# Later LSTM weights fetched and summed eight gates behind a change of phase, and a group's second output one gate later

## The chip, the cores and the metric

The kernel runs as one launch on one core of a Trainium2 chip. The metric is the device time of one execution in microseconds, given as the median of several runs. Beside it stands a profile of one execution, with every engine's instructions and every DMA.

## The reference, cut to what matters

The program has four layers on x of 128 × 64 × 256 float32, which is 8192 tokens of 256 features. Each layer is normalised first (layer norm, then ReLU) and added to its input. The change lies in layer 0, which runs two graph convolutions and then an LSTM over windows of p = 1, 2, 3 and 4 neighbouring nodes, each p with weights of its own:

```python
for p in range(1, MAX_SKIP + 1):
    nw = Tv // p
    wins = h[:, :nw * p, :].reshape(Bv * nw, p, Hd)
    last = _lstm_last(Wih[p - 1], Whh[p - 1], bih[p - 1], bhh[p - 1], wins)
    idx = jnp.arange(nw) * p + (p - 1)
    h = h.at[:, idx, :].set(last.reshape(Bv, nw, Hd))
# _lstm_last, one step:
g = x_t @ Wih.T + h @ Whh.T + bias
i, f, gg, o = jnp.split(g, 4, axis=-1)
c = sigmoid(f) * c + sigmoid(i) * tanh(gg)
h = sigmoid(o) * tanh(c)
```

The window p + 1 reads what the window p has written. Layer 1 (attention over the edges of a graph) takes the sum of x and layer 0's output; layers 2 and 3 follow.

## The kernel before

**Groups, halves, phases.** The 8192 tokens are four groups g = 0 to 3 of 2048. A group's hidden state lies feature-major in SBUF in `hTs0[g % 2]`, so two groups are there at once: half 0 is groups 0 and 1, half 1 is groups 2 and 3, whose states wait in DRAM (`hmem`, in the trace `hm8` to `hm15`, chunks of 512 tokens). For each half the windows w = 1 to 4 run in turn. That makes eight phases (0 to 7), of 12, 28, 22 and 30 gates per half, 184 gates in all. The loop at L820 to L882 goes over these gates, one "slot" each.

**A gate.** A product of a gate's weights with the inputs (and, from the second step of a window on, with the hidden state) is computed with seven instead of eight block products, in the manner of Strassen. This needs sums of weight blocks and sums of input blocks. `Weights` (L424) fetches one window's `Wih` or `Whh` by a DMA on SP's queue (1 MB) and forms its sums by four `tensor_tensor` on GpSimd (L440, tiles `sih` and `shh`). The `ih` weights have two buffers, the `hh` weights one. `prepare` (L617) forms the sums of inputs in tile `xop`: on VectorE L623, L628 and L629 for w = 1; on ACT L632 and L633 and on VectorE L634, L640 and L641 for the other windows.

`gate` (L686) is a generator that gives TensorE the products in four parts. The PSUM tiles are `pa` (three buffers), `pc` (three) and `pb`, which takes one of the two buffers named `bank`. Three gates are interleaved: in a slot TensorE runs products 1 and 2 of the new gate, 3 and 4 of the gate two slots older, 5 of the last one, and 6 and 7 of the new one. VectorE adds the products together at L695 (`pb`), L710 (`pc` of the oldest) and L705 (`pa` of the last gate), in the order in which they are written; product 3 of a gate waits for the L705 of the same gate. `gate_done` follows with the element-wise LSTM (L728, L729, L737, L750 and their neighbours).

**At the change of a phase.** The loop calls `phase_over(ph)` (L806) two slots behind the last gate of phase `ph`. It creates the next phase's `hh` weights at once, if there are any to be used (w = 1 has none), and puts the `ih` weights of phase `ph + 2`, which take the buffer that has just come free, on the list `later_weights` with a due slot eight gates later. When that slot comes, L865 creates them.

**Program order and the scheduler.** The order of instructions on an engine isn't only the order in which the program is written: a scheduler may move an instruction ahead of others on its queue when nothing binds it. `late` (L71) calls `tc.keep_in_program_order` and pins an instruction behind everything written before it on that engine. The weights of L865 aren't pinned in this kernel, so that their DMA and sums are moved up to the change of phase itself: the trace has eight sums in a row there, four `sih` and four `shh`, with the `ih` fetch ahead of the `hh` fetch.

**Output of a group.** When the last step of w = 4 of a group is done, its output is due in two parts, c = 0 and c = 1 (L882). `group_out(g, c)` (L779) transposes 2 × 512 tokens on TensorE (L167, 16 transposes into the two `bank` buffers), adds them to x in tile `xres` on VectorE (L172, four adds), stores the two chunks of the sum by DMAs on GpSimd's queue (`xa`), and for the first half reloads the freed part of `hTs0` with the other half's state from `hmem` by SP (L789). x itself has been fetched by `fetch_x` on SP (`xres` from x). It is called in the part of the loop that runs only when there is a new gate; what is still due behind the last gate goes into `last_outs` (L883). Layer 1 then fetches the x chunks for what is left in `last_outs` (L919), behind the DMAs of its own first weights (`wlv`, L914 to L916, and `wout`), and `edges(q)` (L1281) calls one `group_out` in each of its first steps.

**Layer 2's weights** (`layer2_weights`, L927) are fetched during layer 1: `w1T` by SP and its sums by GpSimd in `quarter_sums` (L126), beside the layer norms of layer 1, whose roots (L99 to L102) also run on GpSimd and whose scaling (L109) runs on ACT.

Of the kernel before, what the change touches and what calls it, by code (L numbers as in the profile page):

```python
# [13 lines left out]
ALU = mybir.AluOpType  # L14
# [3 lines left out]
T = 64  # L18
# [12 lines left out]
def gnn_stack_kernel(ctx: ExitStack, tc: tile.TileContext, a: dict, out: bass.AP):  # L31
    nc = tc.nc
# [45 lines left out]
    class Norm:  # L78


        def __init__(self, xt, root_on_scalar=False, keep=late):
            self.xt, self.root_on_scalar, self.keep, self.h = xt, root_on_scalar, keep, None
            self.st = stat.tile([P, 4, 6], F32, tag="ln_st", name="ln_st")
            self.mv = stat.tile([P, 4, 2], F32, tag="ln_mv", name="ln_mv")
# [170 lines left out]
    keep = tabs.tile([P, E], F32, tag="keep", name="keep")  # L255
# [159 lines left out]
    with ExitStack() as l0:  # L415
# [6 lines left out]


        class Weights:  # L424
            def __init__(self, kind, w):
                bufs = 2 if kind == "ih" else 1
                t = wsp.tile([P, 2, 4, 2, P], F32, tag=f"w{kind}", name=f"w{kind}", bufs=bufs)
                s = wsp.tile([P, 3, 4, P], F32, tag=f"s{kind}", name=f"s{kind}", bufs=bufs)
                nc.sync.dma_start(
                    out=t.rearrange("p k q j m -> p k (q j m)"), in_=a[f"W{kind}T"][:, w - 1]  # L430
                )
                a11, a12, a21, a22 = t[:, 0, :, 0, :], t[:, 1, :, 0, :], t[:, 0, :, 1, :], t[:, 1, :, 1, :]
                s1, s2, s4 = s[:, 0], s[:, 1], s[:, 2]
                for o, x, y, op in (
                    (s1, a21, a22, ALU.add),
                    (s2, s1, a11, ALU.subtract),
                    (s4, a12, s2, ALU.subtract),
                    (a21, a11, a21, ALU.subtract),
                ):
                    nc.gpsimd.tensor_tensor(o, x, y, op)  # L440
                self.of = {1: a11, 2: a12, 3: s4, 4: a22, 5: s1, 6: s2, 7: a21}

            def __call__(self, k, q):
# [6 lines left out]
        weights = {}  # L450


        with ExitStack() as conv:
# [43 lines left out]
            p = bank()  # L497
# [97 lines left out]
        class Step:  # L595
# [21 lines left out]
            def prepare(self):  # L617

                N, t = self.N, self.t
                x = xop.tile([P, 7 * NMAX], F32, tag="x", name="xop")  # L620
                if self.w == 1:
                    v = x[:, : 4 * N].rearrange("p (q n) -> p q n", n=N)
                    nc.vector.tensor_tensor(  # L623
                        v[:, 0:2], self.nodes(slice(2, 4), 0), self.nodes(slice(0, 3, 2), 0), ALU.subtract
                    )
                    b11, b21, b22 = (self.nodes(slice(k, k + 1), 0)[:, 0] for k in (0, 1, 3))
                    nc.vector.tensor_tensor(v[:, 2], b22, v[:, 0], ALU.subtract)
                    nc.vector.tensor_tensor(v[:, 3], b21, v[:, 2], ALU.subtract)  # L628
                    self.x = {1: b11, 2: b21, 3: b22, 4: v[:, 3], 5: v[:, 0], 6: v[:, 2], 7: v[:, 1]}  # L629
                    return  # L630
                v = x[:, : 7 * N].rearrange("p (q n) -> p q n", n=N)
                nc.scalar.copy(self.as_nodes(v[:, 0:2]), self.nodes(slice(0, 2), t))  # L632
                nc.scalar.copy(self.as_nodes(v[:, 2:3]), self.nodes(slice(3, 4), t))  # L633
                nc.vector.tensor_tensor(  # L634
                    self.as_nodes(v[:, 3:5]),
                    self.nodes(slice(2, 4), t),
                    self.nodes(slice(0, 3, 2), t),
                    ALU.subtract,
                )
                nc.vector.tensor_tensor(v[:, 5], v[:, 2], v[:, 3], ALU.subtract)  # L640
                nc.vector.tensor_tensor(v[:, 6], v[:, 1], v[:, 5], ALU.subtract)  # L641
                self.x = {1: v[:, 0], 2: v[:, 1], 3: v[:, 2], 4: v[:, 6], 5: v[:, 3], 6: v[:, 5], 7: v[:, 4]}

            def product(self, q, targets):
# [112 lines left out]
        steps, phases = [], []  # L757
        for half in range(2):
            ga, gb = 2 * half, 2 * half + 1
            for w in range(1, MAX_SKIP + 1):  # L760
                ph = len(phases)
# [55 lines left out]
        later, outs = [], []  # L817
        norm_steps = iter(())
        steps[0].prepare()
        for slot in range(len(tasks) + 2):  # L820
            new = tasks[slot] if slot < len(tasks) else None
            if slot == len(tasks):

                for _ in norm_steps:
                    pass
                first_hT = gp.tile([P, 4 * NMAX], F32, tag="gate", name="hT1_first")
                first_hT = first_hT[:, : 2 * CHUNK].rearrange("p (c t) -> p c t", c=2)
                for ip in range(2):
                    transpose_features(norms1[0].h, first_hT, ip, late)
            if new:  # L830
                step = steps[new[0]]
                one = step.gate(new[1])
                next(one)
            if len(flight) > 1:
                old = flight.pop(0)
                next(old[1], None)
                next(flight[-1][1])
            elif flight and not new:
                old = flight.pop(0)
                next(old[1], None)  # L840
            else:
                old = None
                if flight:
                    next(flight[-1][1])
            if new:
                next(one)
                flight.append((new, one))
                at, k = new[0], new[2]
                while outs and outs[0][0] <= slot:
                    group_out(*outs.pop(0)[1:])  # L850

                new_half = at + 1 < len(steps) and at and steps[at + 1].w == 1 < step.w
                if k == len(step.gates) - (1 if new_half else 2) and at + 1 < len(steps):
                    steps[at + 1].prepare()
                if step.w == MAX_SKIP and step.t == 2 and k < 2 and step.g < NGR - 1:
                    for u in range(2):
                        n = 4 * step.g + 2 * u + k
                        later.append((slot, "x", n))
            while later and later[0][0] <= slot:
                _, kind, n = later.pop(0)  # L860
                residual[n] = fetch_x(n)
            next(norm_steps, None)
            while later_weights and later_weights[0][0] <= slot:
                _, ph = later_weights.pop(0)
                weights["ih", ph] = Weights("ih", phases[ph])  # L865
            if old:
                (at, q, k), step = old[0], steps[old[0][0]]
                if k == len(step.gates) - 1:
                    if at + 1 == len(steps) or steps[at + 1].phase != step.phase:
                        phase_over(step.phase)  # L870
                    if step.phase == len(phases) - 1 and step.t == 1 and step.g == NGR - 1:

                        t_ = wsp.tile([P, 2, 4, 2, P], F32, tag="wih", name="x_first", bufs=2)
                        flat = t_.rearrange("p k q j m -> p k (q j m)")
                        norms1 = {}
                        for n in range(2):
                            xt = flat[:, n, :].rearrange("p (i d) -> p i d", i=4)
                            nc.sync.dma_start(out=xt, in_=xa[n])
                            norms1[n] = Norm(xt)
                        norm_steps = first_norms1(norms1)  # L880
                    if step.w == MAX_SKIP and step.t == MAX_SKIP - 1:
                        outs += [(slot + 1, step.g, 0), (slot + 2, step.g, 1)]  # L882
        last_outs = [(g, c) for _, g, c in outs]  # L883
    psums["banks"] = None

# [2 lines left out]
    with ExitStack() as l1:  # L888
# [306 lines left out]
        def sums(n, xt, keep=False):  # L1195

            st = stat.tile([P, 4, 6], F32, tag="ln_st", name="ln_st")
            mv = stat.tile([P, 4, 2], F32, tag="ln_mv", name="ln_mv")
            for i in range(4):
                ins = nc.vector.bn_stats(st[:, i, :], xt[:, i, :])  # L1200
                if keep and i == 0:
                    late(ins)
                nc.vector.bn_aggr(mv[:, i, :], st[:, i, :])
            rs, nm = w12t["x_rs"][:, n, :], w12t["x_nm"][:, n, :]
            ins = nc.gpsimd.tensor_scalar(rs, mv[:, :, 1], 1e-5, None, ALU.add)
            if keep:
                late(ins)
            nc.gpsimd.tensor_tensor(rs, rs, half_power, ALU.pow)
            nc.gpsimd.tensor_tensor(nm, mv[:, :, 0], rs, ALU.mult)
            nc.gpsimd.tensor_scalar(nm, nm, -1.0, None, ALU.mult)  # L1210
# [158 lines left out]
    with ExitStack() as l2:  # L1369
# [273 lines left out]
        for k in range(2):  # L1643
            f = t4.tile([P, 4, P], F32, tag=f"field{k}", name=f"field{k}", bufs=1)
# [348 lines left out]
```

## Time and profile before

| | |
|---|---|
| median of three runs | 2067.21 us (2066.95 to 2071.63) |
| the profiled execution, its own time | 2061.03 us |
| its span | 2059.3 us |
| mean granted TensorE clock | 0.996 |
| graph convolutions of layer 0 | up to about 190 us |
| LSTM | about 190 to 1273 us |
| layer 1 | about 1273 to 1660 us |
| GpSimd's weight sums in the LSTM (stretches) | 273.4–279.5, 408.5–422.6, 560.8–573.8, 742.4–752.5, 817.45–822.6, 953.9–967.9, 1107.1–1112.5 us |
| a group's outputs | about 724–757 (groups 0 and 1), 1257–1267 (group 2), behind 1273 (group 3) |

Two kinds of view are used below. In a table of windows each row is a stretch of the span: its bounds, its length, then for each engine its busy time and in brackets how many instructions it has run, at the end TensorE's granted clock (1.00 is full speed), the share of the time in which the DMA engines were busy, and the rate of transfer. In a timeline each row is one instruction or a few equal ones in a row: start in us, duration, engine, line of the program, operation, output and inputs with their shapes, and in brackets how long the engine had been idle before it and what released it. PEld is the load of weights into TensorE, which overlaps with its matmuls. The times of the profiled execution are from the start of its span; its own time is 6.2 us (0.3%) under the median of the runs.

### The profile page before, as it was taken

The page shows a single profiled execution, that of the slowest core. Times are in us where ns is not written, and L with a number is a line of the kernel's source. Part 1 is how long each engine was busy: PE and PEld are TensorE (multiplying, and loading weights), DVE is VectorE, ACT ScalarE, POOL GpSimd, SP SyncE. Part 2 cuts the span into 40 slices and gives each one's busy share as a digit, 9 for nine tenths or more (in the row PEclk, how much of TensorE's full clock was granted, in tenths as well). Part 3 has the DMA queues.
Part 4 walks back from the last instruction along what each step waited for, and adds up shares of the span by engine and source line. Part 5 has one row for each costly group of instructions (what it writes and reads, how often), then busy time and mean ns, then how long its engine had stood idle before and what let it go on. Part 6 is the DMA issues. An engine that isn't in the chain of part 4 may idle for free. (4 is left out here: it accounts for less than half of the span.)

```text
span 2059.3 us, 25491 instructions
## 1 busy us (share of the span) xinstructions
PE 2006.1 (97%) x9444; PEld 1346.1 (65%) x9444; DVE 1359.5 (66%) x2507; ACT 1184.4 (58%) x2230; POOL 308.2 (15%) x416
## 2 busy tenths in 40 slices
PE   8999999999999999999999999999999999999998
PEld 6777478866688845887667887333334775444786
DVE  8755666564565477566556555677777877886776
ACT  4344766555565457566446564666675556591544
POOL 3000010020110020002001000323223420000563
PEclk9999999999999999999999999999999999999999
DMA  9331000100100170001001003412223841022012
GB/s 316 98 98 51 0 21 1 42 0 1 41 1 1 40 246 21 1 0 42 0 1 41 1 16 120 138 61 97 72 98 122 298 154 52 0 82 82 32 62 72
DMA packets 63196, 135.06 MB, mean 66 GB/s; under 512 B 6240, under 2 KB 40928, under 8 KB 60768
## 3 DMA queue, kind: packets, MB, share of 16 engines
q1 hardware_dynamic: 56832, 109.11, 15.6%
q0 software_dynamic: 5632, 24.12, 3.1%
q8 instruction: 74, 1.21, 0.2%
q14 instruction: 50, 0.41, 0.1%
q10 hardware_dynamic: 608, 0.20, 0.0%
HBM read 87.28 MB, written 46.14 MB: 65 GB/s over the span
## 5 line engine op out<-in xcount | busy, mean ns | idle before, releaser
L651 PE MATMUL pa<-xop,sih 128*128 128x256 f32 (+2 forms) x1056 | 344.4, 418 | 11.7 <-DVE gate L705 8.2
L679 ACT ACTIVATE gate<-gate,bias 128x256 f32<-128x256 f32 (+2 forms) x368 | 247.4, 679 | 173.6 <-DVE gate L695 91.0
L651 PEld LDWEIGHTS pa<-xop,sih 128*128 128x128 f32 x1056 | 198.4, 190 | 87.9 <-issue 22.8
L651 PE MATMUL pc<-xop,wih 128*128 128x256 f32 (+2 forms) x736 | 251.2, 423 | 0.0
L695 DVE TENSOR_TENSOR gate<-pb,gate 128x256 f32<-128x256 f32 (+2 forms) x184 | 87.5, 475 | 225.7 <-PE pb L651 154.1
L651 PE MATMUL pa<-lstm_h,shh 128*128 128x256 f32 (+1 forms) x672 | 212.7, 398 | 0.0
L993 DVE SCALAR_TENSOR_TENSOR lr<-lr 128x1024 f32<-128x1024 f32 x128 | 151.1, 1222 | 55.3 <-ACT lr L992 55.3
L651 PEld LDWEIGHTS pc<-xop,wih 128*128 128x128 f32 x736 | 139.8, 190 | 51.2 <-issue 23.0
L710 DVE TENSOR_TENSOR gate<-pc,gate 128x256 f32<-128x256 f32 (+2 forms) x184 | 87.6, 476 | 121.2 <-PE pc L651 120.9
L992 ACT COPY lr<-pair 128x1024 f32<-128x1024 f32 x128 | 123.1, 1014 | 47.6 <-PE pair L986 47.6
L651 PEld LDWEIGHTS pa<-lstm_h,shh 128*128 128x128 f32 x672 | 127.7, 190 | 30.2
L651 PE MATMUL pc<-lstm_h,whh 128*128 128x256 f32 (+1 forms) x448 | 141.8, 398 | 0.0
L694 ACT COPY gate<-pa 128x256 f32<-128x256 f32 (+2 forms) x184 | 76.1, 413 | 96.7 <-PE pa L651 96.1
L986 PE MATMUL pair<-sd_hot,xq 64*128 64x512 f32 x512 | 127.5, 616 | 0.3 <-ACT lr L992 0.3
L705 DVE TENSOR_TENSOR gate<-pa,gate 128x256 f32<-128x256 f32 (+2 forms) x184 | 87.5, 475 | 44.0 <-PE pa L651 43.4
L970 PE MATMUL bank<-wlv,hT 128*128 128x512 f32 x240 | 110.7, 604 | 0.0
L699 ACT COPY gate<-pa 128x256 f32<-128x256 f32 (+2 forms) x184 | 75.4, 410 | 59.1 <-PE pa L651 57.9
L679 ACT ACTIVATE gate<-pa,bias 128x256 f32<-128x256 f32 (+2 forms) x184 | 94.0, 511 | 23.6 <-PE pa L651 22.0
L440 POOL TENSOR_TENSOR sih<-wih 128x512 f32<-128x512 f32 x8 | 10.7, 1335 | 630.6 <-DMA wih<-in_WihT 484.4
L651 PE MATMUL pa<-xop,wih 128*128 128x256 f32 (+1 forms) x320 | 101.4, 398 | 2.7 <-ACT xop L632 2.7
L651 PE MATMUL pb<-xop,wih 128*128 128x256 f32 (+1 forms) x320 | 100.3, 398 | 0.4 <-DVE gate L695 0.4
L651 PEld LDWEIGHTS pc<-lstm_h,whh 128*128 128x128 f32 x448 | 85.1, 190 | 20.1
(346 smaller groups left out, 3809.2 us busy)
## 6 DMA issues: line engine op xcount, KB each, us to landing
field<-sd_hot SPq DMA_DIRECT2D x4, 2304.0 KB, 17.2
wih<-in_WihT SPq DMA_DIRECT2D x8, 1024.0 KB, 5.1
xres<-in_x SPq DMA_DIRECT2D x16, 512.0 KB, 4.6
xa<-xres POOLq DMA_DIRECT2D x16, 512.0 KB, 5.2
dense<-field POOLq DMA_DIRECT2D x4, 2048.0 KB, 8.5
xin<-xb SPq DMA_DIRECT2D x16, 512.0 KB, 3.4
h<-xb SPq DMA_DIRECT2D x16, 512.0 KB, 3.2
xin<-in_x SPq DMA_DIRECT2D x15, 512.0 KB, 3.9
```

The costliest lines, as they stand in the source:

```text
L440: nc.gpsimd.tensor_tensor(o, x, y, op)
L651: ins = nc.tensor.matmul(p[:, : self.N], weights[kind, self.phase](k, q), x[k], start=first_ and kind == "ih", stop=kind == "hh" or not se ...
L679: nc.scalar.activation(out, in_, AF.Tanh if q == 2 else AF.Sigmoid, bias=bias[:, self.w - 1, 2 * q + j : 2 * q + j + 1],)
L694: nc.scalar.copy(blk[0, 0], pa[:, :N])
L695: nc.vector.tensor_tensor(blk[0, 0], pb[:, :N], blk[0, 0], ALU.add)
L699: nc.scalar.copy(blk[1, 0], pa[:, :N])
L705: nc.vector.tensor_tensor(blk[1, 1], pa[:, :N], blk[1, 1], ALU.add)
L710: nc.vector.tensor_tensor(blk[1, 0], pc[:, :N], blk[1, 0], ALU.add)
L970: ins = nc.tensor.matmul(p, hTs[n][:, k, i * P : (i + 1) * P], wlv[:, k, :], start=k == 0, stop=k == 1)
L986: ins = nc.tensor.matmul(p[:, par, :], queries[it][r, c * P : (c + 1) * P], sd_hot[r, :], start=True, stop=True)
L992: nc.scalar.copy(lr, p)
L993: nc.vector.scalar_tensor_tensor(lr, lr, 0.2, lr, ALU.mult, ALU.max)
```

## The change

The diff, with the alias in `prepare` (`copy, sums = nc.scalar.copy, nc.vector.tensor_tensor`, used for the same five calls in the same order) left out:

```diff
         class Weights:
-            def __init__(self, kind, w):
+            def __init__(self, kind, w, keep=lambda ins: None):
...
-                nc.sync.dma_start(
-                    out=t.rearrange("p k q j m -> p k (q j m)"), in_=a[f"W{kind}T"][:, w - 1]
+                keep(
+                    nc.sync.dma_start(
+                        out=t.rearrange("p k q j m -> p k (q j m)"), in_=a[f"W{kind}T"][:, w - 1]
+                    )
                 )
...
-                    nc.gpsimd.tensor_tensor(o, x, y, op)
+                    keep(nc.gpsimd.tensor_tensor(o, x, y, op))
...
                 _, ph = later_weights.pop(0)
-                weights["ih", ph] = Weights("ih", phases[ph])
+                weights["ih", ph] = Weights("ih", phases[ph], late)
...
                     if step.w == MAX_SKIP and step.t == MAX_SKIP - 1:
-                        outs += [(slot + 1, step.g, 0), (slot + 2, step.g, 1)]
+                        outs += [(slot + 1, step.g, 0), (slot + 3, step.g, 1)]
```

First, the `ih` weights that L865 creates are pinned where the program has them: their SP DMA and their four GpSimd sums stand eight gates behind `phase_over`. Six sets are concerned, those of phases 2 to 7; the weights of phases 0 and 1 and all `hh` weights are as before. Nothing is added or dropped in number: 24 sums and 6 DMAs change places. At each change of phase the `hh` fetch and its sums come first now.

Second, a group's second output is due three slots behind its last gate's completion instead of two. For group 0 its transposes move behind the first gate of the new half, its adds on VectorE behind L729 and ahead of L628; with them move its two stores and its reload of `hTs0`. For group 1 they move by one gate, the adds behind L737 and L623. For group 2 the due slot falls behind the last new gate, so that this output stays in `last_outs` with the two of group 3: three calls of `group_out` are left for layer 1 instead of two, at q = 0, 1 and 2, and group 3's two come one step later each. Its two chunks of x are fetched again at L919 (SP's fetches into `xres` go from 16 to 18).

The order of the queues changes around this: the two fetches of x into `xres` that wait for stores of group 2's first output stand ahead of `wlv` and `wout` on SP; `w1T` of layer 2 stands behind a load of layer 1's input and is created behind one more output; its GpSimd sums stand ahead of and among the roots (L99, L100) of the norm for chunk 3.

## The prediction

> **What bounds the kernel.** The page's first part comes first: TensorE is busy for 97% of the span. I then cut the LSTM stretch into windows and read TensorE's idle time as length less busy time.
>
> ```profile
> PE 2006.1 (97%) x9444; PEld 1346.1 (65%) x9444; DVE 1359.5 (66%) x2507; ACT 1184.4 (58%) x2230; POOL 308.2 (15%) x416
> ...
> 285.00:404.00 119.00, 118.94 (x547) 103.56 (x547) 67.53 (x127) 71.45 (x152) 0.00 (x0) 1.00 0.00 1
> 404.00:428.00 24.00, 21.82 (x76) 13.79 (x75) 21.61 (x33) 17.52 (x32) 13.92 (x8) 1.00 0.23 88
> 556.00:580.00 24.00, 19.72 (x85) 15.28 (x85) 21.70 (x36) 16.95 (x33) 12.82 (x8) 1.00 0.23 88
> 712.00:736.00 24.00, 20.55 (x89) 14.45 (x88) 13.85 (x21) 7.68 (x15) 2.38 (x4) 0.93 0.77 246
> 736.00:765.00 29.00, 27.85 (x92) 14.33 (x91) 21.80 (x29) 17.82 (x27) 12.06 (x12) 1.00 0.70 246
> 810.00:830.00 20.00, 18.23 (x78) 13.94 (x77) 18.44 (x36) 16.29 (x35) 5.05 (x4) 1.00 0.16 53
> 949.00:974.00 25.00, 22.83 (x80) 14.42 (x79) 22.42 (x34) 18.43 (x33) 13.85 (x8) 1.00 0.22 85
> 1101.00:1121.00 20.00, 17.20 (x76) 13.51 (x75) 18.12 (x34) 15.31 (x31) 5.33 (x4) 1.00 0.28 106
> 1255.00:1320.00 65.00, 63.43 (x304) 33.49 (x305) 42.22 (x63) 34.40 (x58) 16.28 (x22) 1.00 0.56 192
> ```
>
> Columns: stretch, its length, busy time of PE, PEld, DVE, ACT, POOL, granted clock, DMA share, GB/s. Inside a phase (row 285:404) TensorE idles 0.06 us of 119 and VectorE works 57%. The idle time sits at the changes of phase, of half, and of layer: 2.18, 4.28, 3.45, 1.15, 1.77, 2.17, 2.80, 1.57 us in the eight rows below. With 0.86 at 268:285 that is 20.2 us, the most this change could touch. Who ends each wait, from the timeline (start, length of one, engine, line, tiles, count, idle before and its releaser):
>
> ```profile
> 713.28 2.16 SPq L789 DMA_DIRECT2D hT<-hm  x2
> ...
> 720.61 1.23 DVE L623 TENSOR_TENSOR xop<-hT 128x1024 f32<-128x1024 f32 x1 [3.48 <-DMA hT<-hm]
> ...
> 724.89 1.25 PE L167 MATMUL bank<-ident,hT 128*128 128x128 f32 x8 [3.10 <-DVE xres L172]
> ...
> 756.05 1.25 PE L167 MATMUL bank<-ident,hT 128*128 128x128 f32 x8 [0.80 <-DVE xres L172]
> ...
> 570.55 2.10 DVE L634 TENSOR_TENSOR xop<-hT 128x512 f32<-128x512 f32 x1
> ...
> 824.91 0.68 DVE L634 TENSOR_TENSOR xop<-hT 128x512 f32<-128x512 f32 x1
> ...
> 971.63 0.83 PE L651 MATMUL pa<-xop,sih 128*128 128x336 f32 x2 [1.56 <-DVE gate L705]
> ```
>
> Two different things are to be seen. An output's transposes (L167) wait at 724.89 for VectorE's adds (L172) to free one of two banks. And the same L634 takes 2.10 us while GpSimd sums weights, 0.68 us when it does not.
>
> **A. Second output of group 0, one gate later.** Before: 3.27 us of stall at 724.89, then 3.40 us (726.2 to 729.6) at a granted clock of 0.51, whose work at full clock would take 1.73, so 1.67 more: 4.9 in all. After: the transposes stand behind the new half's first gate; VectorE's four adds then queue behind two L728/L729 operations of about 1.22 each, so the third bank comes about 1.65 late (0.5 to 3). The output also issues the half's last reload of hT. Issued near 730.7 and landing 5.6 later as the row at 713.28 did (waited for until 720.61, plus store time), it comes at 736.3; VectorE's L623 wants it near 733.7, and behind L623 queue L695, L710, L705, which TensorE waits for. L705 then ends about 738.6, wanted at 738.4: +0.2 (0 to 3). Gain 4.9 − 1.65 − 0.2 ≈ **−3.1** (−4.5 to +1).
>
> Here a rule is weighed. The Trainium skill, "TensorE: Matmul & The Clock Gate", section on the HAM clock gate, has the array slow down after a fully idle window of roughly 3.4 us that runs free, so an idle of 3.10 need not cool it; by the rule alone only 3.27 would be won and A is −1.4. The row shows a clock of 0.51 directly behind the 3.10; I take the row. If the new 1.65 stall cooled it too, A would be about −1.4 again; no 1.5 us stall elsewhere did (clock 1.00 at 556:580).
>
> **B. Second output of group 1.** Before 0.80 at 756.05. After, its adds stand behind L737 and L623 on VectorE (1.2 each): stall ≈ 2.3, **+1.5** (−0.8 to +2).
>
> **C. Groups 2 and 3.** Group 2's second output falls due after the last gate, so it is left over: it runs in layer 1, and so do group 3's two, each one step later. Away go stalls at the LSTM's end, 2.83 us of transposes with their waits (1264.21 to 1267.04) and 0.59 at 1271.47; added in layer 1: 16 transposes at the rate there, 2.2 (1.9 to 2.4). **−1.2.** Its two 512 KB chunks of x are fetched again.
>
> **D. SP's queue at the layer change.** Two x fetches that wait for stores of group 2 now stand ahead of the layer's first weights (before: issued at 1227). The store at 1257.90 let its fetch go at 1260.98, the second at 1262.55; so the weights go at about 1263.1 and 1263.7 and land at an estimated 1268.5 to 1269.3 (wih took 5.1 for 1 MB; these are half that or less each, behind 1 MB of x). Their first user in before:
>
> ```profile
> 1273.30 3.60 PE L970 MATMUL bank<-wlv,hT_first 128*128 128x512 f32 x8
> ```
>
> About 3 us of transposes ahead of it are gone, so it wants them near 1270: **+0.3** (0 to 2.5). Layer 2's w1 now goes later too, about 1304 for 1295.94, and GpSimd's sum of it stands ahead of a norm's roots (L99); the norm's scaling on ACT comes about 1 us late against a slack of 0.35 in front of TensorE's pair bank: **+0.7** (0 to 2.5).
>
> **E. Weight fetch and sums leave the phase changes.** Six groups of one 1 MB fetch and four GpSimd sums (1.27 us each) go to the eighth gate behind; none is added. What disappears is counted from windows with and without them.
> - 810:830 holds four of the moved sums alone: L641 at 817.59 took 1.41 us beside a sum and 0.42 without, and 0.9 of the stall goes.
> - 404:428 and 949:974 hold eight (four moved, four of whh that stay and now come first): the waits of .38/.39 and 1.73 end on operations stretched by the moved ones, −1.8 each with the first .55 staying.
> - 556:580 (eight) becomes like 1101:1121 (four of whh alone): 4.28 to 2.80, taken as −1.0, because there the remaining four still meet L634.
> - 268, 736 and 1101: nothing.
>
> Sum **−5.5** (−3 to −7).
>
> The second rule speaks against this. The Trainium skill, "SBUF — State Buffer", section "Who interferes with whom", has certain VectorE instructions with two SBUF inputs and a GpSimd instruction exclude each other for whole instructions. The trace agrees: L634 2.10 = 0.70 + about 1.40, operations with a PSUM input (L695, L705: 0.41) unchanged. So moving removes no collision: by the rule four sums of 1.28 put up to 5.1 us on VectorE wherever they land, six groups 30.7 us. What decides is VectorE's slack there: 43% in row 285:404. The nearest row for landing is 736:765, eight sums at 742 to 752, where VectorE's operations were not longer and TensorE's only stall among them was the .51 that steps always have. I take 0.15 a group, **+0.9** (0 to 12.7, rival 3).
>
> **Sum.** −3.1 + 1.5 − 1.2 + 0.3 + 0.7 − 5.5 + 0.9 = −6.4 us on the profiled execution's 2061.03 (span 2059.3). The median of the runs, 2067.21, lies 6.2 above it, so the saving is set against the median: **2060.8 us**, −0.31%. A measurement of this kernel tells about 0.3% (6.2 us) from no change, so the forecast lies on that border.
>
> **Rivals.**
> 1. *The reload, the layer weights or w1 take A and C back.* DMA is at 0.77 in 712:736, and three chains have under 1 us of slack by my working; against it, each has a landing row that just fits. A, B, C, D then give 0 together, E and its landing −4.6: 2062.6. If all of that and half of E fails: 2065.
> 2. *The sums cost as much where they land.* For it: the exclusion rule and the stall of 1.73 at 971.63. Against it: VectorE's slack there. E and landing 0, the rest −1.8: 2065.4.
> 3. *Slower.* The landing gate is one where L641/L634 stand directly ahead of L705, so each of six groups costs what 964.71 and 971.63 did together, .39 + 1.73 = 2.1. Then +12.7 − 5.5 − 1.8 = +5.4: 2072.6. It decides from 1.2 us a group ((5.5 + 1.8)/6). Against it beside the slack: only one gate in 3 or 4 prepares a new step, and a group's sums (5 us) cover less than one gate (184 gates in some 1083 us, 5.9 each).
> 4. *All of it pays.* A 4.9 without a new stall, E 7, landing free: −12, 2055.
> 5. *It does not do what it says.* For the third group this is so already: its output is not one gate later but in another layer, with x fetched twice; counted in C and D.
>
> **Chances.** Forecast case (2058 to 2062) 0.37; rival 4 and its neighbourhood 0.18; rival 1 0.18; rival 2 0.14; rival 3 0.13. Faster by over 0.3% (under 2061.0): most of rival 4, two thirds of the forecast, a little of rival 1, 0.50. Within: 0.37. Slower: 0.13. Range 2054.5 to 2069.
>
> **What would show it.** After: at 712:736 a clock of 1.00 and no L167 wait over 2 us; L623 of the new half waiting under 1 us on hT; the four sih sums some ten gates behind each phase change, and TensorE's idle time in that window within 0.3 us of row 285:404; 810:830 under 1 us idle, 404:428 and 949:974 near 0.5; L970's first matmul not waiting for wlv. Wrong if any moved group costs TensorE over 1.2 us, if a stall over 2.5 us stands on hT, wlv or xres, or if the clock falls at another place.

## The result and the profile after

The median is 2072.53 us for the changed kernel against 2070.03 us for the kernel before, 17 runs each; the ratio is 1.0011, with a 95% interval from 1.0004 to 1.0017. So the change costs 2.3 us or 0.1%, where 6.4 us less were forecast. In a second measurement the ratio was 1.0014 (1.0007 to 1.0020), so that the loss is small, but both intervals lie above 1. One run of the changed kernel, 2140.17 us at a mean clock of 0.944, is left out of the ratio. The forecast of 2060.8 stood on a median of 2067.21 from three runs of the kernel before; its 17 runs here give 2070.03, so 2.8 us of the distance from 2060.8 to 2072.53 are not the change's. The profiled execution took 2073.39 us, with a span of 2071.6.

The table of windows after, in the columns of the one shown before:

```profile
404.00:428.00 24.00, 21.54 (x75) 13.60 (x74) 21.74 (x32) 17.21 (x31) 13.56 (x8) 1.00 0.23 88
556.00:580.00 24.00, 19.60 (x84) 15.13 (x83) 21.68 (x35) 16.43 (x33) 13.45 (x8) 1.00 0.23 88
712.00:740.00 28.00, 25.07 (x103) 17.21 (x102) 16.81 (x25) 10.09 (x20) 2.39 (x4) 0.94 0.65 217
740.00:770.00 30.00, 27.85 (x88) 13.76 (x87) 22.44 (x30) 17.67 (x27) 7.10 (x8) 1.00 0.63 217
810.00:830.00 20.00, 18.47 (x78) 13.95 (x77) 18.44 (x34) 16.33 (x32) 5.11 (x4) 1.00 0.15 53
949.00:975.00 26.00, 23.83 (x85) 15.37 (x84) 23.09 (x36) 18.96 (x34) 13.84 (x8) 1.00 0.21 82
1101.00:1121.00 20.00, 17.02 (x73) 13.14 (x72) 18.09 (x31) 14.61 (x28) 5.25 (x4) 1.00 0.28 106
1255.00:1320.00 65.00, 63.86 (x307) 34.24 (x305) 41.34 (x63) 31.81 (x54) 14.13 (x22) 1.00 0.54 182
1320.00:1326.00 6.00, 3.47 (x12) 1.19 (x8) 3.26 (x6) 4.48 (x7) 0.00 (x0) 0.72 0.69 261
```

The fifth figure with its count is GpSimd. There are still eight sums at 404:428, 556:580 and 949:975, and four at 810:830: **five of the six sets that were to move have not left the changes of phase.** TensorE's idle time there is 2.46, 4.40, 2.17 and 1.53 us, for 2.18, 4.28, 2.17 and 1.77 before. The last row is new: 2.53 us of idle time in layer 1 and a granted clock of 0.72. Before, there was nothing:

```profile
1320.00:1326.00 6.00, 6.00 (x24) 2.87 (x22) 5.16 (x10) 3.73 (x7) 0.04 (x1) 1.00 0.06 24
```

The timeline of the changed kernel at the first of these changes of phase (L442 is L440 of the kernel before, L637 is L634, L708 is L705):

```profile
409.22 1.28 POOL L442 TENSOR_TENSOR shh<-whh 128x512 f32<-128x512 f32 x1 [129.60 <-DMA whh<-in_WhhT]
...
414.41 2.59 POOL L442 TENSOR_TENSOR sih<-wih 128x512 f32<-128x512 f32 x1
...
417.15 2.17 DVE L637 TENSOR_TENSOR xop<-hT 128x672 f32<-128x672 f32 x1
...
420.44 2.58 POOL L442 TENSOR_TENSOR wih<-wih 128x512 f32<-128x512 f32 x1
...
426.71 0.83 PE L654 MATMUL pa<-xop,sih 128*128 128x336 f32 x2 [1.56 <-DVE gate L708]
```

The same place before:

```profile
416.73 2.17 DVE L634 TENSOR_TENSOR xop<-hT 128x672 f32<-128x672 f32 x1
...
426.29 0.83 PE L651 MATMUL pa<-xop,sih 128*128 128x336 f32 x2 [1.56 <-DVE gate L705]
```

The four of whh come first, as the new order says. The four of wih follow at once and stretch L637 to 2.17 us, as those of whh, which came last before, did with L634; the stall of 1.56 is there to the hundredth. GpSimd had been idle for 129.60 us: with nothing on its queue that could hold it, a pinned operation runs as soon as its weights land. The pin says behind what it stands on its own queue, and the gates that it was meant to trail run on other engines. So the early start needs no moving by the scheduler, to which the text on the kernel before puts it down.

The exception is the change of half. There the pinned fetch stands on SP's queue behind two reloads of hT that wait themselves (L792), so it is issued at 765.21 (736.90 before), and the sums run from 774.50 (742.42 before):

```profile
761.58 3.58 SPq L792 DMA_DIRECT2D hT<-hm  x2
765.21 0.88 SPq L430 DMA_DIRECT2D wih<-in_WihT  x1
...
774.50 1.27 POOL L442 TENSOR_TENSOR sih<-wih 128x512 f32<-128x512 f32 x1 [7.99 <-DMA wih<-in_WihT]
```

TensorE idles for 0.00 us from 773 to 784. Here something ahead on the same queue did take time, and the pin did delay.

A stage-by-stage account needs one more view, of the change and of the experiments that follow. Each row takes the same operation (the nth L705 of the gates, the nth L993 of layer 1's edges) in two traces and gives how much later it starts than in the profile of before.

| us later than before at | 626 | 693 | 793 | 940 | 1271 (LSTM's end) | 1312 | 1328 | 1562 |
|---|---|---|---|---|---|---|---|---|
| change, first profile | 0.55 | 0.55 | 1.71 | 1.21 | −1.66 | 0.89 | 5.10 | 5.10 |
| change, second profile | 1.39 | 1.39 | 0.22 | −0.01 | −3.07 | −0.51 | 0.61 | 0.61 |
| pin only | 0.44 | 0.44 | −0.10 | −0.23 | −0.14 | −0.14 | −0.14 | −0.14 |
| later output only | −0.67 | −0.67 | 2.64 | 2.52 | −0.78 | 1.77 | 2.89 | 2.89 |
| later output, groups 0 and 1 | −0.14 | −0.14 | 1.09 | 1.08 | 1.26 | 1.26 | 1.26 | 1.26 |
| held sums, eight gates | −4.79 | −4.79 | −3.57 | −3.36 | −5.38 | −5.38 | −5.38 | −5.38 |
| change, w1's sums behind the norm | 0.70 | 0.70 | −0.50 | −0.80 | −3.47 | −0.91 | −0.91 | −0.91 |
| the same, and held | −3.96 | −3.96 | −3.98 | −3.70 | −8.71 | −6.15 | −6.15 | −6.15 |
| held, third group alone later | −4.56 | −4.56 | −4.32 | −4.08 | −9.04 | −6.49 | −6.49 | −6.49 |
| group 0 alone later | −0.50 | −0.49 | 0.43 | 0.49 | 0.23 | 0.22 | 0.23 | 0.23 |
| held sums, three gates | 10.89 | 10.89 | 11.06 | 16.08 | 19.66 | 19.66 | 19.66 | 19.66 |
| before, second profile | 1.45 | 1.45 | 1.25 | 1.24 | 0.40 | 0.40 | 0.40 | 0.40 |

The last row says how finely it can be read: the kernel before differs from itself by 1.7 us at 303, ahead of the changes of phase, and by up to 0.8 between columns. The change's first profile loses at three places: the change of half (693 to 793), the third output in layer 1 (1271 to 1312: 2.55), and 1312 to 1328 (4.21). It wins 3.0 at the LSTM's end.

The half's change, in the timeline of the changed kernel (L731 and L732 are L728 and L729 of before):

```profile
728.07 1.23 DVE L731 TENSOR_TENSOR gate<-gate,lstm_c 128x1024 f32<-128x1024 f32 x1 [1.10 <-ACT gate L682]
729.33 1.23 DVE L732 TENSOR_TENSOR lstm_c<-gate 128x1024 f32<-128x1024 f32 x1
...
731.21 1.59 PE L167 MATMUL bank<-ident,hT 128*128 128x128 f32 x8 [2.34 <-DVE xres L172]
...
763.35 1.26 PE L167 MATMUL bank<-ident,hT 128*128 128x128 f32 x8 [1.80 <-DVE xres L172]
```

The adds stand behind L731 and L732 as forecast, but L731 itself waited 1.10 us for ACT, so that the stall is 2.34 us and not 1.65. And 1312 to 1328:

```profile
1305.83 0.34 SPq L934 DMA_DIRECT2D w1T<-in_W1T  x1
...
1313.45 1.27 POOL L136 TENSOR_TENSOR w1S<-w1T 128x256 f32<-128x256 f32 x1 [5.74 <-DMA w1T<-in_W1T]
...
1314.81 1.08 POOL L99 TENSOR_SCALAR ln_rs<-ln_mv 128x4 f32<-128x4 f32 x1
...
1317.92 1.05 POOL L100 TENSOR_TENSOR ln_rs<-ln_rs,half_power 128x4 f32<-128x4 f32 x1
...
1319.60 2.07 ACT L109 ACTIVATE h<-xin,ln_nm,ln_rs 128x256 f32<-128x256 f32 x4 [2.82 <-POOL ln_nm L102]
...
1322.62 3.60 PE L989 MATMUL pair<-sd_hot,xq 64*128 64x512 f32 x8 [2.53 <-ACT lr L995]
```

Read downwards this is one chain. w1T lands 7.6 us after its issue; GpSimd's first sum waits for it, the norm's L99 stands behind that sum and its L100 behind three more; ACT's L109 waits 2.82 us for the norm, ACT's next copy stands behind L109, and TensorE waits 2.53 us for the copy. L973 of layer 1's first weights starts at 1271.64 without a wait.

### The profile page after: what moved, and what is told of

The parts are those of the page before. It is cut to its first block, busy times and chain, and to the rows that moved or that the text cites. A ratio compares the mean times of both kernels' runs of the same rounds, so it can differ in the third digit from the quotient of the medians.

```text
span 2071.6 us, 25484 instructions
## 1 busy us (share of the span) xinstructions
PE 2013.5 (97%) x9444; PEld 1349.5 (65%) x9444; DVE 1360.7 (66%) x2507; ACT 1183.1 (57%) x2230; POOL 308.4 (15%) x416
## 3 DMA queue, kind: packets, MB, share of 16 engines
q8 instruction: 74, 1.21, 0.2%
## 5 line engine op out<-in xcount | busy, mean ns | idle before, releaser
L708 DVE TENSOR_TENSOR gate<-pa,gate 128x256 f32<-128x256 f32 (+2 forms) x184 | 87.4, 475 | 43.7 <-PE pa L654 43.1
L973 PE MATMUL bank<-wlv,hT 128*128 128x512 f32 x240 | 110.7, 604 | 0.0
L989 PEld LDWEIGHTS pair<-sd_hot,xq 64*128 64x128 f32 x512 | 44.2, 188 | 74.8 <-issue 36.0
```

The lines of the kernel that those rows point to most:

```text
L708: nc.vector.tensor_tensor(blk[1, 1], pa[:, :N], blk[1, 1], ALU.add)
L973: ins = nc.tensor.matmul(p, hTs[n][:, k, i * P : (i + 1) * P], wlv[:, k, :], start=k == 0, stop=k == 1)
L989: ins = nc.tensor.matmul(p[:, par, :], queries[it][r, c * P : (c + 1) * P], sd_hot[r, :], start=True, stop=True)
```

## The experiments

"Theory Q" in the expectations is what the first profile suggested: the pin does nothing in time, and the later output carries the loss. "Theory P" is the prediction. Each ratio is against the kernel before in the same measurement on the same chip. Its median was 2061.58 us for the pin alone, the later output alone, groups 0 and 1, and the sums held for eight gates, and 2069.8 to 2070.0 us for the others.

**The pin alone.** The changed kernel, with the output's due slot back at 2:

```diff
-                        outs += [(slot + 1, step.g, 0), (slot + 3, step.g, 1)]
+                        outs += [(slot + 1, step.g, 0), (slot + 2, step.g, 1)]
```

> Only the pinning of the later ih weights; outputs as in the kernel before. Theory Q (a pin orders a queue and holds nothing back in time: GpSimd has nothing to do there, so the pinned sums still run as soon as the weights land, and only swap places with the sums of whh): the four sih sums start within 15 us of the change of phase, as in the changed kernel, and the time is that of the kernel before within 1 us (about +0.5 us, the 0.55 by which the changed kernel is late at 700 us). Theory P (the prediction's part E): the sums come some ten gates behind the change of phase and the time falls by 4.6 us.

Ratio 1.0004 (0.9995 to 1.0012), and −0.14 us at the LSTM's end. Theory Q holds: the pin alone is worth nothing that can be measured. Five sets start within 15 us of their change of phase; the one at the change of half starts at 768.59, later than Theory Q said.

**The later output alone**, on the kernel before (slot + 2 to slot + 3, weights unpinned).

> Only the second output one gate later, weights as in the kernel before. Theory Q: it carries nearly all that the change does. Group 0 and 1 at the change of half about +0.7 us, the LSTM's end and the third output in layer 1 together -0.5, the late w1 with its stall in front of the pair bank and the clock behind it +4.2: about +4.4 us in a profile, the stall at about 1322. Theory P (prediction, A to D): -2.8 us.

Ratio 1.0025 (1.0018 to 1.0032), 2.89 us late at 1562. The later output carries the loss. The stall near 1322 was only 1.00 us here, without a slow clock behind it; the half's change cost more (3.3), with stalls of 2.33 and 3.06:

```profile
763.00 1.25 PE L167 MATMUL bank<-ident,hT 128*128 128x128 f32 x8 [3.06 <-DVE xres L172]
```

This is dearer than the whole change (intervals 1.0018 to 1.0032, and 1.0004 to 1.0017). What the change has in addition is the pin, and the one place where it moves sums is here: without it the sums of wih run from 749.5 to 756.6 and stretch the two L731 ahead of group 1's output to 2.22 and 1.69 us; with it these take 1.22 each (L734 there), and the stall is 1.80. A run with only this set pinned was not made, and part of the 3.3 us is a clock of 0.5 behind each of the two stalls.

**The later output for groups 0 and 1 only:**

```diff
-(slot + 2, step.g, 1)
+(slot + (3 if step.g < 2 else 2), step.g, 1)
```

> Second output one gate later for groups 0 and 1 only; group 2 stays at the LSTM's end and layer 1 gets two outputs as before. Theory Q: no stall over 1 us in front of the pair bank near 1320, two outputs in layer 1, w1T issued near 1296; the time +0.7 us on before (-1 to +2). Theory P: A and B alone, -1.6 us.

Ratio 1.0004 (0.9995 to 1.0012). At the half's change 1.2 us are lost, and there is no stall in front of the pair bank: that one comes with the third group's output in layer 1.

**Sums that are really held.** Pinned as in the change, but behind a small operation that cannot run before the gate is done (output's due slot at 2):

```diff
                 _, ph = later_weights.pop(0)
+                sight = gp.tile([P, 4], F32, tag="sight", name="sight", bufs=2)
+                late(nc.gpsimd.tensor_scalar(sight, steps[old[0][0]].act[old[0][1]][-1][:, -4:], 1.0, None, ALU.mult))
                 weights["ih", ph] = Weights("ih", phases[ph], late)
```

> The pinning plus one tiny GpSimd operation ahead of each set of sums that reads the gate just finished, so that the sums really start at the eighth gate behind the change of phase. Outputs as in the kernel before. If the prediction's working of the phase changes was right and only the delay was missing: stalls at 410-428, 815-830 and 949-974 shrink by 0.9 to 1.8 us each and the time falls by about 4.6 us on before (5.5 less 0.9 at the landing places). If sums cost the same wherever they run (exclusion with VectorE): within 1 us of before. If they cost 2.1 us a set where they land: +7 us.

Ratio 0.9972 (0.9962 to 0.9982): 2055.71 us against 2061.58 on the same chip. Windows of this kernel at two changes of phase and at three places where sums now run:

```profile
404.00:428.00 24.00, 24.00 (x85) 15.49 (x84) 20.81 (x34) 19.02 (x35) 6.61 (x4) 1.00 0.23 88
446.00:458.00 12.00, 12.00 (x44) 8.07 (x43) 5.61 (x8) 4.74 (x9) 6.50 (x5) 1.00 0.00 1
556.00:580.00 24.00, 21.17 (x94) 17.18 (x93) 20.20 (x36) 18.47 (x37) 6.02 (x4) 1.00 0.16 68
589.00:600.00 11.00, 11.00 (x53) 9.68 (x52) 5.69 (x8) 5.05 (x11) 6.26 (x5) 1.00 0.00 0
790.00:802.00 12.00, 11.79 (x28) 4.94 (x26) 10.31 (x12) 8.61 (x15) 7.54 (x5) 1.00 0.00 1
```

TensorE's idle time at 404:428 goes from 2.18 to 0.00 and at 556:580 from 4.28 to 2.83. The fetches still go out at the changes of phase (the second at 404.18), so what cost the time there were the sums and not the fetch. Where the sums land (446:458, 589:600) VectorE is busy for half the time and TensorE idles 0.00; at 790:802, in a w = 1 phase with VectorE at 86%, it idles 0.21. The same view of the other three landing places shows TensorE idle for 0.00 too. The timeline shows the holding operation at work:

```profile
448.30 0.22 POOL L869 TENSOR_SCALAR sight<-gate 128x4 f32<-128x4 f32 x1 [32.62 <-ACT gate L682]
...
448.49 2.55 POOL L442 TENSOR_TENSOR sih<-wih 128x512 f32<-128x512 f32 x1
```

GpSimd had been idle for 32.62 us, and what released it is ACT's gate, no DMA. This one operation is all that sets the kernel apart from the pin alone.

**Held three gates instead of eight** (`later_weights.append((slot + 3, ph + 2))`).

> Held sums, but three gates behind the change of phase instead of eight; outputs as in the kernel before. If it matters only that the ih sums leave the change of phase itself, this is as good as eight (-5.4 us on before). If the first gates of a new phase are still tight on VectorE, it gets back part: -3 to -5, with stalls where the sums run.

Ratio 1.0087 (1.0073 to 1.0100): worse than any other kernel here, by 18 us on before, and outside both expectations. One of its landing places, the window and then the timeline:

```profile
420.00:436.00 16.00, 12.19 (x34) 7.25 (x33) 13.22 (x17) 8.39 (x15) 7.48 (x5) 0.81 0.00 0
```

```profile
424.80 1.92 DVE L755 TENSOR_TENSOR lstm_h<-lstm_h 128x672 f32<-128x672 f32 x1
...
426.64 1.57 DVE L644 TENSOR_TENSOR xop<-xop 128x336 f32<-128x336 f32 x1
...
431.42 1.49 PE L654 MATMUL pa<-xop,sih 128*128 128x336 f32 x2 [3.81 <-DVE gate L708]
```

Three gates on, the first steps prepare `lstm_h` and `xop` for the second ones, and these are VectorE operations with two SBUF inputs. At this place in the kernel that holds for eight gates they took less than half as long:

```profile
419.93 0.85 DVE L755 TENSOR_TENSOR lstm_h<-lstm_h 128x672 f32<-128x672 f32 x1
420.70 0.50 DVE L644 TENSOR_TENSOR xop<-xop 128x336 f32<-128x336 f32 x1
```

TensorE idles 3.81 us and the clock falls to a mean of 0.81. In the view of the table this costs 3.1 to 5.0 us on the kernel before at five of the six sets, and 4.1 to 6.7 us on the kernel that holds for eight gates. The sixth, at the change of half, costs nothing.

**The change once more.**

> The changed kernel unchanged, for a second profile and a ratio beside the others. Theory Q: 5.1 us late on the profile of before at 1330 us as in its first profile (LSTM and first steps of layer 1 repeat), with the 2.5 us stall and the slow clock near 1322; the 5 us by which layer 1 lost more near 1587 to 1594 (matmuls in bursts of five with 0.4 us between) do not come again if they are an event of one execution, and come again if the change makes them. Ratio 1.001 to 1.0025.

It ends at 0.61 us where the first profile had 5.10. At the half's change, windows of the first profile and then of the second:

```profile
728.00:732.00 4.00, 1.66 (x14) 1.24 (x13) 3.75 (x5) 2.05 (x4) 0.00 (x0) 1.00 0.37 130
732.00:736.00 4.00, 4.00 (x10) 2.19 (x10) 1.31 (x3) 0.58 (x1) 1.07 (x2) 0.58 0.68 212
```

```profile
728.00:732.00 4.00, 1.72 (x13) 1.22 (x11) 3.63 (x4) 2.33 (x4) 0.00 (x0) 1.00 0.32 111
732.00:736.00 4.00, 4.00 (x18) 2.78 (x17) 2.00 (x4) 1.30 (x3) 1.07 (x2) 1.00 0.71 235
```

Much the same stall (2.34 and 2.28) was followed by a clock of 0.58 in one execution and 1.00 in the other. And w1T landed 4.9 us after its issue instead of 7.6, which leaves a stall of 1.00 and no slow clock:

```profile
1319.69 2.04 PE L989 MATMUL pair<-sd_hot,xq 64*128 64x512 f32 x8 [1.00 <-ACT lr L995]
```

So the first profile shows the dearer form of both losses; a stretch near 1587 came again and is taken up with the second profile of before.

**w1's sums behind the norm.** The changed kernel with `layer2_weights` called at q = 3 and its sums pinned:

```diff
+            if q == 3:
+                layer2_weights()
             if q == 1:
 
                 l0out.close()
-                layer2_weights()
```

> The changed kernel with layer 2's w1 weights created two steps later and their GpSimd sums pinned, so that they stand behind the roots of the norm for chunk 3 instead of ahead of and among them. Theory W (w1's late landing holds up that norm): the stall near 1322 and the clock of 0.51 behind it go, edge 18 of layer 1 comes 4.2 us earlier than in the changed kernel, leaving +0.9 us on before. Rival (the third output's adds or its transposes hold up the norm): the stall stays over 2 us.

```profile
1315.00:1320.00 5.00, 5.00 (x32) 1.47 (x28) 2.55 (x3) 4.36 (x7) 0.30 (x1) 1.00 0.98 362
1320.00:1322.60 2.60, 2.60 (x8) 1.25 (x7) 2.46 (x7) 1.71 (x4) 0.00 (x0) 1.00 0.55 214
```

There is no stall, and nothing is lost from 1312 to 1328 (−0.91 in both columns). w1T itself was issued at 1304.03, much as in the two profiles of the change (1305.83 and 1304.43), and its first sum began 6.5 us later, more than the 4.9 that came with a stall of 1.00. What changed is the order on GpSimd, where the norm's roots now stand ahead of the sums, and that was the cause. Ratio 1.0001 (0.9992 to 1.0009).

**Both mended**: the same with held sums.

> The changed kernel, sums held by a small GpSimd operation that reads the finished gate, w1 later. This is the change with both of its failures mended: the parts measured so far add up to -5.2 (held sums) + 0.7 (groups 0 and 1) - 0.5 (third output in layer 1) = -5.0 us on before. If parts collide where they meet (change of half), up to -3.5.

Ratio 0.9972 (0.9961 to 0.9982), −6.15 us in the table.

**The best one**: as the last, but only the third group's output late.

```diff
-(slot + 3, step.g, 1)
+(slot + (3 if step.g == 2 else 2), step.g, 1)
```

> Held sums, w1 later, third group's second output in layer 1, but the second outputs of groups 0 and 1 as in the kernel before. Parts: -5.4 - 0.5 = -5.9 us on before; 0.5 to 1.5 us less than the held sums with a later output for all groups.

Ratio 0.9964 (0.9950 to 0.9977), 2062.56 us against 2069.95: faster than both kernels, by 7.4 us on the one before. The interval overlaps those of the other two held kernels, so the order among the three isn't settled.

**Group 0's output alone** (`3 if step.g == 0 else 2`).

> Only group 0's second output one gate later: part A alone. From the profiles of the change: a stall of 2.3 to 2.5 us at about 730 in place of 3.27 at 724.89, with or without a slow clock behind it (seen with it in the change's first profile and without in its second). So -0.8 to -2.4 us on before behind the change of half, against the -3.1 of the prediction; group 1's stall stays near 0.8.

Ratio 0.9998 (0.9991 to 1.0005). The stall at 730 was 2.33 with a clock of 1.00 behind it, as expected, but the gain of 0.8 to 2.4 us was not there: 0.9 us were lost up to 793, since group 1's output, which was not moved, now stalls too, with a clock of 0.5 behind it. This kernel has the line numbers of before, where L731 is the first step's product:

```profile
749.80 2.10 DVE L731 TENSOR_TENSOR gate<-gate 128x1024 f32<-128x1024 f32 x1
...
754.78 1.25 PE L167 MATMUL bank<-ident,hT 128*128 128x128 f32 x8 [2.17 <-DVE xres L172]
```

In the kernel before the eight sums were over at 752.5 and L731 began at 752.44, at 1.22 us each. Here the gates are 2.6 us ahead, and the four sums of wih, now behind the stores of the moved output, run until 755.3 and stretch L731. What an output gains at one place can be lost where it pushes other work together.

**The kernel before once more.**

> The kernel before, unchanged, for a second profile. If the 5 to 6 us lost near 1587 in the second profile of the change and in those with w1 later are the chip's and not the change's, they show here too when the runs of before on this chip lie near 2070 us, and they do not when these lie near 2061. If they belong to the change, they show in no profile of before, wherever it runs. Ratio 1.000.

```profile
1582.16 0.34 PE L1158 MATMUL pair<-att,xv_in 64*64 64x64 f32 x5 [0.37 <-issue]
...
1584.76 5.19 PE L1180 MATMUL bank<-wout,yT 128*128 128x256 f32 x16
```

Ratio 0.9995 (0.9987 to 1.0004). The short matmuls in bursts of five, with waits for nothing that the profile shows, and the slow L1180 behind them (3.72 us in the first profile of before) are in the kernel before too. They cost 5.1 us here (0.40 to 5.49 in the view of the table, from 1562 to 1600; 5.1 to 6.8 in the others), came in each profile taken where before ran near 2070 us, and in none of those taken where it ran near 2061.6; the first profile of before lacks them as well. So the change has no part in them. What makes them was not tried.

## Why the prediction was wrong, point by point

- **E, the step that failed.** "Six groups of one 1 MB fetch and four GpSimd sums go to the eighth gate behind." Five of the six don't, and the sixth moves for another reason; the position on GpSimd's queue was read as a time. −5.5 and +0.9 were forecast, nothing was measured (pin alone: 1.0004). The working behind it was right: with the sums really held, TensorE's idle time fell by 2.18 at 404:428, 1.45 at 556:580, 1.39 at 810:830 and 1.77 at 946:972, where 1.8, 1.0, 0.9 and 1.8 (at 949:974) were forecast, landing cost 0.00 five times of six, and at the LSTM's end 5.4 us were gained where 4.6 net were forecast.
- **Its reading of the waits** is slightly high. .55, .39 and 1.73 add up to 2.67 at 949:974, where the window has 2.17 and the timeline shows waits of 0.38, 0.23 and 1.56; the 3.27 at 724.89 is 3.10 in the same way.
- **The fifth rival**, that the change doesn't do what it says, was the true one, and was given no chance of its own; it was looked for in the third group and not in the pin.
- **The exclusion rule and the third rival.** VectorE's slack did decide, as the text said, and eight gates was a place with enough of it. The row that was taken as the nearest for landing, 736:765, could not show it: the VectorE operations beside its sums (L710, L705, L172, L695) each have an input from PSUM, and these are the ones that the sums leave alone (L710 took 0.69 us among them at 743.35, and 0.68 without a sum at 758.80 of the kernel with the later output alone). The third rival's price of 2.1 us was, if anything, low: three gates on it is 3.1 to 5.0. It decides by the place, which the change never reached.
- **A and B** were −1.6 together. From 693 to 940, the three profiles with the pin and both outputs late give +0.66, −1.40 and −1.50, the two without the pin +3.19 and +1.22, and the one with held sums +0.26. Where the clock stayed at 1.00 (−1.40 and −1.50) the sum was nearly met, in part by luck: the new stall is 2.3 us and not 1.65, since L731's own wait for ACT was left out, and group 1's is 1.80 and not 2.3. In the other four the clock fell behind one or two of the stalls; the forecast had counted that loss as gone, and had named it as a risk. The reload that was feared made VectorE wait for hT by 0.74 us in the first profile and 2.43 in the second, and TensorE not at all.
- **The clock rule.** The row was preferred to the rule and the row held: stalls of 2.71 to 3.50 us at the half's change were followed by about half the clock in all seven cases (before twice, pin alone, later output alone, held for eight and for three gates, best one).
- **C** was −1.2 and measures −0.5: −3.0 at the LSTM's end (−2.7 to −3.3 over four profiles), since the stall of 0.59 stayed, and +2.55 for the third output.
- **D**: wlv 0 (forecast +0.3). w1 +4.2 in one profile and +1.1 in two others (forecast +0.7, at most 2.5). The chain was the one described; its size depends on how long w1T takes to land, 4.9 or 7.6 us (4.4 in the profile of before), for which the forecast had no spread, and the clock behind the stall had no term at all.

With E at nothing the forecast's other terms come to −1.8 us, and the ratio says +2.3. The 4.1 us between them are C (0.7), D (0.1 to 3.2) and what the clock did in A and B (up to 2.3), in shares that differ from one execution to the next. The measured ratio lies between what the two profiles of the change come to (−0.4 and +5.0 us, each from its own first gate, at 200 us, to 1562).

## What to carry to other kernels

Position on an in-order queue is a time only if something ahead on that same queue takes or waits for that time, as at the change of half here; to run work later on an idle engine, make it depend on what it is to follow. Work that shares a resource without a wait of its own is priced by the place where it lands: the same four sums cost at most 0.21 us at the eighth gate and 3 to 5 us, but for one place, at the third, so landing places are worth as much study as the place that is left. A small chore on a helper engine's queue ahead of a critical chain's link inherits the chore's own wait for a DMA: put it behind.

## What the runs showed of the hardware

The answer of TensorE's clock to one and the same stall is not fixed. Stalls of 2.17 to 2.34 us at the half's change were followed by a clock of about 0.5 in five of nine cases and by 1.00 in four; the four stalls of 1.80 us at group 1's output in the kernels with the pin and both outputs late were all followed by 1.00. The Trainium skill ("TensorE: Matmul & The Clock Gate", section on the HAM clock gate) calls the window of about 3.4 us free-running, which would fit a stall that is sometimes seen and sometimes not; but it asks for an idle window of that length, and here about 2.2 us between transposes was enough. In the kernel with the sums held for eight gates the clock fell even inside the stall, which began at 717.0:

```profile
719.00:719.20 0.20, 0.00 (x0) 0.00 (x0) 0.20 (x1) 0.00 (x0) 0.00 (x0) 0.98 0.58 97
719.20:719.60 0.40, 0.00 (x0) 0.00 (x0) 0.40 (x1) 0.00 (x0) 0.00 (x0) 0.50 0.56 172
```

That is 2.2 us after the last matmul, and 3.2 us after the start (715.96) of the eight transposes ahead of the stall. Whether transposes count as work for the clock was not tried.

The landing of one DMA varied from 4.9 to 7.6 us for the same w1T in two executions of the same kernel (from its issue to the first sum that waits for it), and with it the stall from 1.00 to 2.53.
